# A macaron network of two layers on one core: zero products in the second layer's entry, another order of its tail, and a dispatch that sums on TensorE

## The chip, the core and the metric

The kernel runs on one core of a Trainium2 chip. A core has five engines, each with its own list of instructions that it works through in order: TensorE (PE; its weight loads are listed as PEld), VectorE (DVE), ScalarE (ACT), GpSimd (POOL) and SyncE (SP), which here only issues DMA transfers. The on-chip memory (SBUF) has 128 partitions; TensorE writes to PSUM, used here as eight banks of 128x512 f32. The metric is the device time of one execution in microseconds (us), lower is better.

## The reference

The input is 1024 tokens of 512 features. Two layers follow, each "macaron": half an FFN, an attention, half an FFN again, each behind a layer norm and added to the residual x.

```python
x = x + 0.5 * L0_ffn(layernorm(x))     # mixture: 16 experts, 4 per token, one shared expert
x = x + L0_attn(layernorm(x))          # 32 heads of 16, causal, rope
x = x + 0.5 * L0_ffn(layernorm(x))
x = x + 0.5 * L1_ffn(layernorm(x))
x = x + L1_attn(layernorm(x))          # one head of 128, all to all
x = x + 0.5 * L1_ffn(layernorm(x))

def L0_ffn(x):                         # sigmoid scores, top 4, normed weights cw
    g, u = x @ Wg[e].T, x @ Wu[e].T    # per expert e, 512 -> 256
    out = sum_e ((silu(g) * u) * cw[e]) @ Wd[e].T
    return out + silu(x @ Sg.T) * (x @ Su.T) @ Sd.T

def L1_ffn(x):
    t = x[:, perm].reshape(1024, 16, 32)          # permuted features, 16 heads
    t = gelu(einsum('bhd,hdm->bhm', t, up))       # 32 -> 128 per head
    t = einsum('bhm,hmd->bhd', t, down)           # 128 -> 32
    return t.reshape(1024, 512)[:, argsort(perm)]

def L1_attn(x):                        # q, k, v of 128, softmax, then Wo
    out = softmax(q @ k.T / sqrt(128)) @ v
    return out @ Wo + bo
```

All of it is in f32 (0/1 masks and zeros in narrower types).

## The kernel before, in words

The tokens are eight tiles of 128 (`NT = 8`), and x stays on chip in `x_sb`. A feature-major copy of the normed x is `xT`, made by four 128x128 transposes per tile (`tr`, line 85) into one bank and one copy out of it (`turned`, by ACT). The work of a stage runs as a hand-written order of small units. TensorE's instructions are pinned to that program order (`mm` at line 82, `tr` at line 85). VectorE, GpSimd and ScalarE are pinned as well in the stretches where `order(True)` was called; the wrapper records all their calls at line 99, so line 99 in a profile row can be any of them, and the tile name tells which. Else a scheduler orders them. `bank()` hands out the eight PSUM banks in turn, so a new bank may have to wait until its last reader is done. `idle(n)` issues n products of zeros (bf16, 128x512) that nobody reads.

**The mixture and its dispatch.** A layer's two mixtures, `m0` before and `m1` after layer 0's attention, both work through 35 blocks of up to 2x64 gathered tokens: `gather`, `turn` (transposes and a copy to `xsT`), `gate_up`, `turn_z`, `down`. Ahead of that, `dispatch` (line 1842) works out which token goes to which place: `choose` marks each token's top 4 (`sel`), `spots_mm` (line 471) counts by products of 0/1 matrices, `before` times one tile's `sel` plus `ones` times all earlier tiles', where the sum over tiles before `lo` is read from `cum` (made by `count`, line 457, one VectorE addition per tile); the last column holds the count over all tiles. `counts` turns it into blocks per expert, `experts` and `experts_row` into the expert of each block (`er`), `bases` (line 625) and `blocks_of` (line 637) into each token's block (`pick`, `qh`, then masks `hb`), `invert` by 32 products into the list of tokens by row (`src_i`), which the gathers need. `weights` makes the weighted masks (`hotw`) and, on ACT, f32 casts `hbf` of `hb`; both are read by `invert_weights`, which runs after the first block's second expert product. `rh` is each token's place in its block. Between these steps stand `pieces`, shares of the shared expert's products, as filler on TensorE; the VectorE product that ends each is the `zs` product, put on the list `later`. `first_step` begins with six zero products, then turns the first block and issues the first expert product. In layer 0 dispatch is called at line 1954 with tiles 4 to 7 still to place, for `m1` at line 2061 with only tile 7 left, in the midst of attention's end. SP's queue in layer 0 carries the loads, the stores of the normed tiles (`xn_d`) and the shared expert's weights (`wsh`, issued in round 6, line 1930).

**Layer 1's entry** (lines 1567 to 1593). GpSimd fetches each token's four rows of the mixture's result (`fetch(t)`, four gathers per tile into `yk`). `enter(t)` issues the fetch of tile t+1, adds three rows to x_t on VectorE, norms tile t-1 (`xn`), adds the fourth row, takes tile t's statistics (with one `pow` on GpSimd, which comes behind the fetch in its queue) and turns tile t-1 into `xT`. `permute(t)` applies the feature permutation by 16 products with a 0/1 matrix `pm` (one permutation in what follows) and copies the result to `xp` on ACT. `permuted(t)` transposes `xp` back and rebuilds x_t from it on VectorE in permuted feature order, since layer 1 up to its last FFN keeps x in that order. For tiles 4 and 5 the permutation goes by memory instead: `send` writes xT to `xd`, and `receive` gathers its rows by four DMAs (`xp<-xd`); its place is inside `enter(7)`, between tile 6's norm and tile 7's last addition.

**Layer 1's FFN** (`Ffn1`, line 1383; `f` first, `f2` last). Its columns come in three groups, `GROUPS = ((0, 4), (4, 6), (6, 8))`: tiles 0 to 3 (512 wide), 4 and 5, 6 and 7 (256 wide, the narrow groups). For a group n and one of four chunks i, `up(n, i)` has four products into four banks and four GELUs into tiles `g` (a ring of 12, shared with the output tile `xo`), and `down(n, i)` four products into one bank and a copy into `yT`. In `f2` a `down` starts with one product per tile of x's own 128x128 block by `ident`, which puts x into the sum. The groups 0 and 1 of `f2` return to the original feature order through memory: `yT` is written to `yd`, `fetch` gathers its rows into `xp` (POOL), `back` transposes; group 2 does it by products with `pmt` (`unpermute`). `store` copies to `xo` and writes out.

**Attention of layer 1** (line 1701). For each query tile: scores, a maximum, `probabilities` (exponentials on ACT), `transposed` (the transposes of the probabilities into `pT`, copied by VectorE and ACT), then per half of four tiles `project` (eight products of values with `pT`, copied as `oT`) and `output` (one product with `wo1` per tile; VectorE adds it to x and `after(t)` norms the tile). `turn` then makes xT of the normed tile for `f2`. The first half's outputs and turns 0 to 3 stand on the list `todo` and are worked off among the second half's steps; in the second half's `project` the hook `between[1]` stands after four of the eight products:

```python
        for u in todo:
            u()
        between[0]()                       # f2.up(0, 0)
        oT = project(pT, between[1])       # 4 products, f2.up(0, 1), 4 products
        between[2]()                       # f2.down(0, 0)
        for tt in range(4):
            output(oT, 1, tt)
```

The functions that the change touches, and what calls them:

## Time and profile before

| what | value |
|---|---|
| time, median of 3 runs (lowest, highest) | 1223.39 us (1221.47, 1229.98) |
| the profiled execution: its own time, and the span of its trace | 1225.28 us, 1223.5 us |
| mean granted TensorE clock in it | 0.982 |
| busy, share of the span: PE, PEld, DVE, ACT, POOL | 94%, 44%, 42%, 38%, 25% |
| stretch 24 to 50 us (dispatch of layer 0): PE, DVE, ACT, POOL busy, clock | 20.81, 20.55, 10.33, 6.32 of 26 us, 0.93 |
| stretch 750 to 768 us (second dispatch) | 15.50, 14.45, 9.62, 4.27 of 18 us, 1.00 |
| stretch 1012 to 1077 us (layer 1's entry) | 54.33, 38.37, 19.11, 42.61 of 65 us, 0.92 |
| stretch 1142 to 1223.5 us (end of the last attention, last FFN) | 70.20, 27.98, 33.49, 12.12 of 81.5 us, 0.96 |

How to read the profile: it is one execution, recorded by the hardware. A group of instructions is a line, an engine, an operation, and what it writes and reads by the program's names. In a timeline row the first number is the start in us from the span's start, the second the time from there to the end of the group, then engine, line, operation and tile, shape, count, and in brackets the engine's idle time before it with what ended it. A row of the waits has the waiting instruction, what it waited for, and the sum of the idle us, the count and the longest. A row of a windows view has the window, its length, then busy us (and instruction count) of PE, PEld, DVE, ACT and POOL, the granted TensorE clock (1.00 is full), the DMA share and GB/s. In the slices of the page each digit is the busy share in tenths of one fortieth of the span. Matmuls are pipelined, and their ends are modelled.

### The profile page before, as it was taken

To read this page: it belongs to the slowest core of one execution; us is meant where nothing else is said; L and a number is where in the kernel's file an instruction comes from. 1 tells how busy PE (TensorE), PEld (TensorE's weight loads), DVE (VectorE), ACT (ScalarE), POOL (GpSimd) and SP (SyncE) were. 2 spreads that over 40 slices of the span, in tenths; PEclk is the share of its full clock that TensorE was granted. 3 is DMA by queue.
4 is the path that set the end of the run, shared out by engine and by line. 5 is a ranking of instruction groups with operands and counts; after the bars stand their busy time and mean duration, and the time that the engine had idled before them with its cause. 6 is when DMAs were issued, how large, how long until landed. Compare 5 with 4: busy or idle time off the path is not lost. (4 is left out here: it accounts for less than half of the span.)

```text
span 1223.5 us, 18918 instructions
## 1 busy us (share of the span) xinstructions
PE 1153.5 (94%) x6570; PEld 536.8 (44%) x6570; DVE 515.9 (42%) x1188; ACT 463.0 (38%) x919; POOL 306.1 (25%) x374
## 2 busy tenths in 40 slices
PE   9899999998979999999989998899998998899898
PEld 6643333336544344444433326434333335565544
DVE  6611111115676574746587206531111115755731
ACT  4312222222245545363655693212222221451544
POOL 5211111105355421211101010431121106642002
PEclk9999999999989999999989999999999998999989
DMA  6644567425331200000000002756246615500004
GB/s 242 240 154 147 180 216 268 165 95 150 93 48 28 39 1 10 10 1 10 10 1 9 10 1 97 260 129 214 88 155 248 217 45 148 163 18 1 1 26 147
DMA packets 41973, 125.02 MB, mean 102 GB/s; under 512 B 6240, under 2 KB 8032, under 8 KB 37776
## 3 DMA queue, kind: packets, MB, share of 16 engines
q1 hardware_dynamic: 15680, 58.38, 14.3%
q0 software_dynamic: 14224, 43.34, 13.0%
q10 hardware_dynamic: 11968, 22.02, 4.8%
q8 instruction: 55, 0.90, 0.3%
q14 instruction: 46, 0.38, 0.1%
HBM read 271.69 MB, written 29.62 MB: 246 GB/s over the span
## 5 line engine op out<-in xcount | busy, mean ns | idle before, releaser
L82 PE MATMUL ps<-wg,xsT 128*64 128x512 f32 x1120 | 257.5, 602 | 10.5 <-DMA wg<-in_w_exp_dram 8.3
L99 DVE TENSOR_REDUCE nm<-ps 128x1 f32<-128x512 f32 (+5 forms) x360 | 195.3, 601 | 76.8 <-PE ps L82 76.2
L82 PE MATMUL ps<-kT,qt 32*128 32x512 f32 (+3 forms) x768 | 166.7, 529 | 3.5 <-DVE nm L99 3.3
L1153 ACT ACTIVATE pt<-ps 128x512 f32<-128x512 f32 x224 | 119.3, 602 | 119.7 <-PE ps L82 119.3
L82 PE MATMUL ps<-qt,kT 32*128 32x512 f32 x576 | 153.5, 651 | 0.5 <-DVE nm L99 0.4
L801 POOL DMA_INDIRECT xs<-xn_d,src_i x70 | 68.2, 974 | 319.3 <-PE ps L85 285.0
L82 PEld LDWEIGHTS ps<-wg,xsT 128*64 128x64 f32 x1120 | 75.7, 137 | 142.9 <-issue 137.5
L82 PE MATMUL ps<-wd,zT 128*64 128x512 f32 x560 | 132.5, 593 | 1.0 <-DVE zT L99 1.0
L99 DVE TENSOR_TENSOR z<-sg,ps 128x256 f32<-128x256 f32 x70 | 29.4, 421 | 243.8 <-ACT sg L99 236.2
L99 ACT ACTIVATE sg<-ps 128x256 f32<-128x256 f32 x70 | 26.9, 384 | 256.3 <-PE ps L82 256.3
L862 ACT ACTIVATE y<-ps,w_row 128x512 f32<-128x512 f32 x70 | 48.1, 687 | 105.3 <-PE ps L82 59.3
L82 PEld LDWEIGHTS ps<-kT,qt 32*128 32x128 f32 x768 | 62.9, 184 | 45.4 <-DVE nm L99 14.9
L99 POOL TENSOR_SCALAR_AFFINE_SELECT pt<-pt 128x512 f32<-128x512 f32 x64 | 41.0, 665 | 165.8 <-ACT pt L1157 155.2
L99 POOL TENSOR_TENSOR rstd<-rstd,mhalf 128x1 f32<-128x1 f32 x40 | 23.7, 594 | 234.7 <-DVE rstd L99 230.0
L82 PE MATMUL ps<-pt,va 128*32 128x512 f32 x576 | 78.7, 612 | 0.0
L82 PEld LDWEIGHTS ps<-wd,zT 128*64 128x64 f32 x560 | 40.6, 137 | 78.6 <-issue 76.5
L99 POOL DMA_INDIRECT yk<-y_d,row_i x48 | 49.2, 1026 | 95.4 <-SPq L914 82.4
L99 DVE COPY zT<-ps 128x256 f32<-128x256 f32 x70 | 29.6, 423 | 102.5 <-PE ps L85 102.4
L82 PEld LDWEIGHTS ps<-qt,kT 32*128 32x128 f32 x576 | 49.3, 187 | 52.4 <-issue 23.8
L82 PE MATMUL ps<-xT,wsh 128*128 128x256 f32 x256 | 60.3, 390 | 4.6 <-PEq L914 3.1
L82 PEld LDWEIGHTS ps<-xT,wsh 128*128 128x128 f32 x256 | 48.3, 193 | 14.3 <-issue 4.5
L85 PEld LDWEIGHTS ps<-ident,xs 128*128 128x128 f32 x280 | 29.4, 141 | 56.7 <-issue 54.4
(265 smaller groups left out, 1468.8 us busy)
## 6 DMA issues: line engine op xcount, KB each, us to landing
wg<-in_w_exp_dram SPq DMA_DIRECT2D x142, 1024.0 KB
wd<-in_w_exp_dram SPq DMA_DIRECT2D x142, 512.0 KB
y_d<-y ACTq DMA_DIRECT2D x70, 256.0 KB
xn_d<-xn SPq DMA_DIRECT2D x16, 256.0 KB
wsh<-in_w_exp_dram SPq DMA_DIRECT2D x2, 1536.0 KB
y_d<-y ACTq DMA_DIRECT2D x2, 1280.0 KB
out_dram<-xo SPq DMA_DIRECT2D x8, 256.0 KB
wqkv_sb<-in_w_qkv_dram POOLq DMA_DIRECT2D x2, 768.0 KB
```

The lines of the kernel that those rows point to most:

```text
L82: pin(nc.tensor.matmul(dst, lhsT=lhsT, rhs=rhs, start=start, stop=stop))
L85: pin(nc.tensor.transpose(dst, src, ident))
L99: ins = f(*a, **k)
L801: nc.gpsimd.indirect_dma_start(out=xs, out_offset=None, in_=self.xn_d, in_offset=bass.IndirectOffsetOnAxis(ap=self.src_i[:, s : s + 1], ax ...
L862: nc.scalar.activation(y, py, AF.Copy, scale=self.w_row[:, s : s + 1])
L1153: nc.scalar.activation(pt, pas[j], AF.Exp, scale=1.0 / 16.0)
```

## The change

Eight edits, in the order in which the kernel runs.

- Dispatch. In layer 0 the four additions `count(0, 4)` go, and TensorE sums `ones` times `sel` over all earlier tiles instead of reading `cum` (`spots_mm(..., summed=False)`); in both layers the sum over all tiles is issued first. The `pick` product of `bases` moves from VectorE to GpSimd and right behind `experts`. The masks `hb` are four instructions instead of two, and stand ahead of one `zs` product. ACT's casts `hbf` move behind `first_step`. One piece instead of two stands ahead of layer 0's dispatch, so one more is left for its end.
- The shared expert's weights are loaded in round 5 instead of 6.
- Entry. 28 zero products instead of 14, eight more after `permute(0)`, two more in each of three rounds.
- `receive()` stands behind tile 7's statistics instead of ahead of its last addition.
- `f2`: x is no longer added by products with `ident`. `raw(t)` transposes x_t into a bank and copies it to `xr` (ACT for even, VectorE for odd tiles), and `down` adds `xr` on VectorE in place of its copy.
- `g` and `xo` share ten buffers instead of twelve.
- `oT` is copied by ACT instead of VectorE.
- The tail's order: ahead of the second half's values stand only the outputs of the first half and `raw(0)`, `raw(1)`; then the eight values products without a hook, turns 0 and 1, the second half's outputs, turns 2 and 3, and from there `f2` with its `raw` units spread among `up` and `down`. The third group's `up` and `down` alternate one step further apart.

```diff
@@ -468,22 +468,24 @@
-        def spots_mm(self, lo, hi):
+        def spots_mm(self, lo, hi, summed=True):
...
             def add(at, hi):
-                mm(at, ones, self.cum[:, lo, :], False, hi == lo)
-                for t in range(lo, hi):
+                if summed:
+                    mm(at, ones, self.cum[:, lo, :], False, hi == lo)
+                for t in range(lo if summed else 0, hi):
                     mm(at, ones, self.sel[:, t, :], False, t == hi - 1)
-            for t in range(lo, hi):
-                at = pos[:, bass.ts(t - lo, E)]
-                mm(at, before, self.sel[:, t, :], True, False)
-                add(at, t)
             if hi == NT:
...
                 add(at, NT - 1)
+            for t in range(lo, hi):
+                at = pos[:, bass.ts(t - lo, E)]
+                mm(at, before, self.sel[:, t, :], True, not (summed or t))
+                add(at, t)
             return pos
@@ -626,27 +628,26 @@
             pick = dp.tile(full, F32, tag="pick", name="pick")
-            vec.tensor_mul(
+            pool.tensor_mul(
                 pick, self.oh, self.base.unsqueeze(1).unsqueeze(2).to_broadcast(full)
             )
+            self.based = pick
+        def blocks_of(self, dp):
             bk = dp.tile([P, TOPK, NT], F32, name="bk")
-            vec.tensor_reduce(bk, pick, AX.X, ALU.add)
+            vec.tensor_reduce(bk, self.based, AX.X, ALU.add)
             self.qh = dp.tile([P, TOPK, NT], FP16, name="qh")
...
-        def blocks_of(self, dp):
-            self.hbs = []
-            full = [P, 2, NT, NH]
-            for i in range(2):
-                hb = dp.tile(full, FP16, name=f"hb{i}")
+            self.hbs = [dp.tile([P, 2, NT, NH], FP16, name=f"hb{i}") for i in range(2)]
+            full = [P, NT, NH]
+            for k in range(TOPK):
                 vec.tensor_tensor(
-                    hb,
-                    iota_h[:, 0:NH].unsqueeze(1).unsqueeze(2).to_broadcast(full),
-                    self.qh[:, 2 * i : 2 * i + 2, :].unsqueeze(3).to_broadcast(full),
+                    self.hbs[k // 2][:, k % 2],
+                    iota_h[:, 0:NH].unsqueeze(1).to_broadcast(full),
+                    self.qh[:, k, :].unsqueeze(2).to_broadcast(full),
                     ALU.is_equal,
                 )
-                self.hbs.append(hb)
@@ -700,7 +701,7 @@
             vec.tensor_reduce(wk, pick, AX.X, ALU.add)
-            self.hotw, self.hbf = [], []
+            self.hotw = []
             full = [P, 2, NT, HB]
@@ -708,6 +709,10 @@
+        def blocks_cast(self, dp):
+            self.hbf = []
+            for i in range(2):
                 hf = dp.tile([P, 2, NT, NH], F32, name=f"hbf{i}")
@@ -1407,7 +1412,7 @@
             for pa in pas:
-                g = self.xpool.tile([P, 512], F32, tag="g", name="g", bufs=12)[:, :w]
+                g = self.xpool.tile([P, 512], F32, tag="g", name="g", bufs=10)[:, :w]
                 nc.scalar.activation(g, pa[:, :w], AF.Gelu)
@@ -1418,21 +1423,20 @@
             pb = bank()
+            for j, g in enumerate(self.gs.pop((n, i))):
+                mm(pb[bass.ts(j, 32), :w], late["down"][:, i * 4 + j, :], g)
             if self.last:
-                lo, hi = GROUPS[n]
-                for t in range(lo, hi):
-                    mm(
-                        pb[:, bass.ts(t - lo, P)], x_sb[:, t, bass.ts(i, P)], ident,
-                        t == lo, False,
-                    )
-            for j, g in enumerate(self.gs.pop((n, i))):
-                mm(pb[bass.ts(j, 32), :w], late["down"][:, i * 4 + j, :], g, not self.last, True)
-            if self.last and n:
-                nc.vector.tensor_copy(yT[:, i, :], pb[:, :w])
+                nc.vector.tensor_add(yT[:, i, :], pb[:, :w], self.xr[:, i, self.cols(n)])
             else:
...
+        def raw(self, t):
+            (nc.vector.tensor_copy if t % 2 else nc.scalar.copy)(
+                self.xr[:, :, bass.ts(t, P)], transposes(x_sb[:, t, :])
+            )
@@ -1464,7 +1468,7 @@
         def store(self, t, ps):
-            xo = self.xpool.tile([P, H], F32, tag="g", name="xo", bufs=12)
+            xo = self.xpool.tile([P, H], F32, tag="g", name="xo", bufs=10)
             (nc.vector.tensor_copy if t % 2 else nc.scalar.copy)(xo, ps)
@@ -1542,7 +1546,7 @@
-            def enter(t, *between):
+            def enter(t):
@@ -1550,11 +1554,11 @@
                     entry_apply(t - 1)
-                for u in between:
-                    u()
                 if t < NT:
...
                     entry_stats(t)
+                if t == 7:
+                    receive()
                 if t > 0:
@@ -1568,13 +1572,15 @@
                 u()
-            idle(14)
+            idle(28)
             enter(1)
             permute(0)
+            idle(8)
             for t in range(2, 5):
...
                 permute(t - 1)
+                idle(2)
             f.up(0, 0)
@@ -1588,7 +1594,7 @@
             f.down(0, 3)
-            enter(7, receive)
+            enter(7)
             permute(6)
@@ -1647,22 +1653,41 @@
         f2 = Ffn1(True, xpool, xT)
+        rp = ctx.enter_context(tc.tile_pool(name="xr", bufs=1))
+        f2.xr = rp.tile([P, KC, S], F32, name="xr")
...
+        def amid():
+            f2.raw(0)
+            f2.raw(1)
+        def turns():
+            turn(0)
+            turn(1)
...
             after,
-            [lambda: f2.up(0, 0), lambda: f2.up(0, 1), lambda: f2.down(0, 0)],
+            [amid, turns],
         )
+        turn(2)
+        turn(3)
+        f2.up(0, 0)
+        f2.raw(2)
+        f2.raw(3)
+        f2.up(0, 1)
+        f2.down(0, 0)
         f2.up(0, 2)
...
         f2.down(0, 2)
+        f2.raw(4)
+        f2.raw(5)
         f2.up(1, 0)
@@ -1671,26 +1696,28 @@
         f2.up(1, 2)
+        f2.raw(6)
         f2.down(1, 1)
         f2.up(1, 3)
+        f2.raw(7)
         f2.up(2, 0)
         f2.down(1, 2)
+        f2.up(2, 1)
         f2.down(1, 3)
         f2.fetch(1, xp)
-        f2.up(2, 1)
+        f2.up(2, 2)
         f2.down(2, 0)
+        f2.up(2, 3)
+        f2.down(2, 1)
         for t in (0, 1):
             f2.store(t, f2.back(t, xp))
-        f2.up(2, 2)
         f2.unpermute(2, 0)
-        f2.down(2, 1)
-        f2.up(2, 3)
+        f2.down(2, 2)
         f2.unpermute(2, 1)
+        f2.down(2, 3)
         for t in (2, 3):
             f2.store(t, f2.back(t, xp))
-        f2.down(2, 2)
         f2.unpermute(2, 2)
-        f2.down(2, 3)
         for t in (4, 5):
@@ -1774,14 +1801,12 @@
-        def project(pT, amid=nothing):
+        def project(pT):
             pb = bank()
...
                 mm(pb, v[:, kt, :], pT[:, kt, :], kt == 0, kt == NT - 1)
-                if kt == NT // 2 - 1:
-                    amid()
             oT = ap2.tile([P, 512], F32, tag="oT", name="oT")
-            nc.vector.tensor_copy(oT, pb)
+            nc.scalar.copy(oT, pb)
             return oT
@@ -1827,19 +1852,19 @@
                     todo.extend([lambda tt=tt: output(oT, 0, tt) for tt in range(4)])
-                    todo.extend([lambda t=t: turn(t) for t in range(4)])
...
         between[0]()
-        oT = project(pT, between[1])
-        between[2]()
+        oT = project(pT)
+        between[1]()
         for tt in range(4):
...
-    def dispatch(m, dp, lo, mid, fill, later, rows):
+    def dispatch(m, dp, lo, mid, fill, later, first, rows):
@@ -1848,11 +1873,12 @@
-        pos = m.spots_mm(lo, NT)
+        pos = m.spots_mm(lo, NT, not first)
         m.choices(mid, NT)
...
         pe = m.experts(dp)
+        m.bases(dp)
         for u in rows:
@@ -1862,10 +1888,9 @@
         m.numbers(lo, NT)
-        m.bases(dp)
         pieces(2)
+        m.blocks_of(dp)
         later.pop(0)()
-        m.blocks_of(dp)
         pieces(3)
@@ -1877,6 +1902,7 @@
         m.first_step()
+        m.blocks_cast(dp)
         m.back_rows(dp)
@@ -1926,7 +1952,7 @@
                     stats(t)
-                if t == 6:
+                if t == 5:
                     m0.load_shared(sp)
@@ -1940,18 +1966,16 @@
             pos = m0.spots_mm(0, 4)
-            m0.count(0, 4)
             compare(6)
...
             choose(6)
-            for _ in range(2):
-                z.pop(0)()
+            z.pop(0)()
...
-            dispatch(m0, dp, 4, 4, z, later, [rows])
+            dispatch(m0, dp, 4, 4, z, later, True, [rows])
             for eng in (vec, pool, act):
@@ -2058,7 +2082,7 @@
             m1.choose(t, NT, m1.compare(t, NT, vec))
-            dispatch(m1, dp, t, t, m1_z[:12], m1_later, [])
+            dispatch(m1, dp, t, t, m1_z[:12], m1_later, False, [])
             del m1_z[:12]
```

## The prediction

> **What bounds the kernel now.** One core, five engines, each running its own list in order. I first read the page's busy shares and slices.
>
> ```profile
> span 1223.5 us, 18918 instructions
> ...
> PE   9899999998979999999989998899998998899898
> ...
> PEclk9999999999989999999989999999999998999989
> ```
>
> TensorE (PE) is busy almost everywhere, so only a stretch where PE idles, runs at a lower granted clock, or does work that can be left out is worth anything. The change touches three: the two dispatches (24 to 50 us and 750 to 768 us), layer 1's entry (1012 to 1077 us) and the tail (1142 us to the end). I read the timeline of each, and the granted clock by windows where PE had idled. First the dispatch of layer 0, on VectorE (DVE), ScalarE (ACT) and PE:
>
> ```profile
> 24.25 1.60 DVE L99 TENSOR_TENSOR cum<-cum,sel 128x16 bf16<-128x16 bf16 x4
> 36.19 0.68 DVE L99 TENSOR_TENSOR pick<-oh,base 128x512 f32<-128x512 bf16 x1
> 46.57 2.41 ACT L99 CAST hbf<-hb 128x1280 f32<-128x1280 f16 x2
> 48.88 0.59 ACT L99 COPY xsT<-ps 128x512 f32<-128x512 f32 x1
> 49.52 3.65 PE L82 MATMUL ps<-wg,xsT 128*64 128x512 f32 x16 [1.54 <-ACT xsT L99]
> ```
>
> The first expert product waits for a copy that stands behind two casts; before that, a chain of small DVE steps decides. Next the clock (PEclk is the third column from the right, after the busy times) and the entry:
>
> ```profile
> 1030.00:1032.00 2.00, 1.33 (x6) 0.93 (x5) 1.77 (x5) 0.58 (x1) 1.39 (x3) 0.50 0.67 209
> 1048.00:1050.00 2.00, 2.00 (x11) 2.00 (x11) 1.93 (x5) 0.00 (x0) 1.39 (x3) 0.50 0.65 213
> 1166.00:1168.00 2.00, 2.00 (x9) 0.50 (x2) 0.00 (x0) 1.14 (x3) 0.00 (x0) 0.50 0.04 8
> ```
>
> ```profile
> 1031.22 6.36 PE L82 MATMUL ps<-xT,pm 128*128 128x128 f32 x32 [0.67 <-issue]
> ...
> 1071.13 0.98 POOL L99 DMA_INDIRECT xp<-xd,pcol  x1 [3.40 <-DMA xd<-xT]
> ...
> 1072.86 3.84 PE L82 MATMUL ps<-xT,pm 128*128 128x128 f32 x32 [0.67 <-ACT xT L99]
> ...
> 1076.51 0.55 DVE L99 TENSOR_SCALAR xn<-x_sb,mvs,rstds 128x512 f32<-128x512 f32 x1 [5.56 <-issue]
> ```
>
> The same permutation takes 6.36 us at clock 0.50 and 3.84 us at 1.00. DVE's waits in 1028 to 1078 us name the victim:
>
> ```profile
> DVE x_sb L99 <- PE ps L85: 7.3, 3, 3.2
> ```
>
> Last, PE's timeline of the tail, and the windows view of 1158.10 to PE's last product (busy PE first):
>
> ```profile
> 1159.16 1.27 PE L85 MATMUL ps<-ident,xn 128*128 128x128 f32 x8 [1.06 <-DVE xn L99]
> 1163.40 1.09 PE L85 MATMUL ps<-ident,xn 128*128 128x128 f32 x4 [2.97 <-DVE xn L99]
> 1165.16 2.09 PE L82 MATMUL ps<-xT,up 32*128 32x512 f32 x8 [0.67 <-ACT xT L99]
> 1167.18 4.91 PE L82 MATMUL ps<-pT,v 128*128 128x512 f32 x8
> ...
> 1173.10 3.70 PE L82 MATMUL ps<-pT,v 128*128 128x512 f32 x8
> ...
> 1187.58 0.66 PE L85 MATMUL ps<-ident,xn 128*128 128x128 f32 x4
> ...
> 1190.96 1.16 PE L82 MATMUL ps<-ident,x_sb 128*128 128x128 f32 x8
> 1158.10:1219.23 61.13, 54.88 (x348) 27.73 (x348) 18.29 (x41) 28.50 (x66) 11.45 (x15) 0.94 0.22 74
> ```
>
> PE waits for four normed tiles, its clock halves, and the next products run at half pace. Afterwards it is the bound.
>
> **Dispatch, layer 0: 2.2 us.** Four additions to cum leave: 1.60 us, stretched while GpSimd (POOL) subtracted at 24.12 to 25.22. The following steps can start at about 24.5 instead of 25.77: 1.2. The sum over all tiles goes first on PE: eight products at 0.027 us instead of nineteen before it: counts start 0.4 sooner. 15 more such products (0.4 us) stand before filler that nobody waits for. The 0.68 us product goes to POOL, where the like 128x512 subtraction took 1.04; DVE's next small steps run just then. A DVE TENSOR_SCALAR of 0.54 us took 1.50 at 1092.70 beside a POOL addition, so I count this move as nothing (between -0.4 and +0.7).
>
> The Trainium skill says the same more strictly ("SBUF — State Buffer", section "SBUF: two separate sides"): the port pair is an exclusive lock, and a DVE instruction with two SBUF inputs or in a two-port mode blocks fully against a reading POOL instruction. The additions' 1.60 us agrees. By the rule the move costs up to 0.4 us, so 1.8 us here instead of 2.2.
>
> One zs product goes behind the block masks: 0.33. The masks come in four parts, so the inversion's last wait covers 8 products and not 16: 0.36. Together 2.3 us earlier at the row numbers. Then PE has six filler pieces instead of five (0.9 each): -0.9; and the xsT copy no longer stands behind the casts (48.88 against PE's end at 48.0): +0.85. About 2.2; I bound it by 0.6 (mask inputs late from ACT, whose table load now stands among them) and 3.0. The casts, 2.41 us, move beside the second expert product (3.65 us); were that cover gone, the weight inversion would wait up to 2.4. The shared weights' DMA passes two stores on SP's queue: it ends a 1.47 us wait of PE that lay beside DVE's chain, and the stores are read 18 us later. Nothing.
>
> Layer 1's dispatch: PE works without a gap from 754.0 through filler and inversion to 764, so the DVE steps saved are hidden, and xsT was copied 0.03 us after its transposes anyhow: 0 (-0.3 to +0.5).
>
> **Entry: 4.5 us.** 28 zero products instead of 14 (14 took 3.25 us) end at 1029.4, inside the 3.03 us that PE waited for xn. Eight more (1.7 us) fall between 1035.1 and the next xn at 1037.0; two per round (0.43) mostly before xn. So the clock should hold: permutation 0 ends at 1035.1 instead of 1037.6, 1 starts at 1038.3 and takes 3.84 where the xp copy came 5.7 us after its start, 2 takes 3.84 instead of 5.47, 3 follows at 1049.5 and not 1053.3. The FFN's first products then start at 1054.0 instead of 1058.56. Is this allowed? POOL issues the yk gathers, 1.28 us apart with one power per tile, without a break until 1051: its pace holds, and tiles up to 4 come no sooner. Tile 5's power moves from 1058.5 to 1057.1, tile 6's from 1066.8 to about 62.6, behind gathers. From 1054.0 ACT is busy for 13.7 us (table 1.28, 16 GELUs at 0.515, copies), so permutation 6 starts at 1068.4 instead of 1072.86: 4.5. The receive (four gathers, behind a 3.40 us wait for xd) now stands after tile 7's power on POOL: DVE's 5.56 us wait goes, worth only 0.4 us on PE. Its first gather lands by 1070 and is needed at 1073. From 1077 to 1128 PE is 51.41 of 51.50 us busy, so the gain passes on. If the 1.8 and 0.8 us by which permutations 1 and 3 were slow at a recorded clock of 1.0 stay: 1.9. The high end is 4.9.
>
> The clock rows come first here: idles of 3.0, 2.0 and 3.0 us were each followed by 3.4 or 6.8 us at 0.50. The skill ("TensorE: Matmul & The Clock Gate", "What's actually happening") puts a re-throttle after one whole idle window of about 3.4 us; here a window only about half busy sufficed, and by the rule alone the 2.0 us idle would not have counted, making the entry gain some 1.5 us smaller.
>
> **Tail: 9.5 us.** The second half's values no longer wait for tiles 0 to 3: two raw transposes fill PE, the last pT copy on DVE is due at 1160.1, values run at full clock to 1167. PE's work from 1158.1 by start-to-start times, before: values 8x0.875, outputs 4x0.87, ups 9.0, downs 8.6, unpermuting 8x0.87, transposes 13x0.44, x products 8.3: 49.1. Idle 61.13-54.88 = 6.25, half clock 2.6 (4.91-3.70, 2.09-1.14, 1.09-0.66), rest 3.2. After: minus 8.3, plus 8 raw transposes 3.5, one output and one turn that come later now 1.3: 45.6. New waits, going through the built order: 0.4 for pT, 1.0 for xT of tiles 2 and 3 behind the outputs, 0.1, and 1.6 where the third hidden group needs a bank that a GELU still holds: 3.1 to 3.6. With a rest of 3.0 to 3.2 PE ends at 1157.8+45.6+3.4+3.1 = 1209.9 instead of 1219.2: 9.3 to 9.5. VectorE's additions (0.69 like its 512-wide copies) replace copies of ACT; the oT copy on ACT starts 0.1 sooner. The yd gathers start 2.7 us after the last yT copy as before, and land 0 to 1 us before they are read. With ten g buffers instead of twelve the third GELU of a narrow group waits for the product after it: about 0.3 us, mostly within PE's pace of 1.4 per pair. Bounds: 6 (ACT paces) to 12.5 (no rest).
>
> **Sum.** 2.2+0+4.5+9.5 = 16.2. The profiled execution took 1225.28 us (span 1223.5, 1.8 around it): 1209.1. The median of the runs, 1223.39, is 1.9 lower: 1207.2. I say 1207.5.
>
> **Rivals.**
> Entry and dispatch hidden (12%): POOL's unbroken gathers speak for it, DVE's 7.3 us of waits against. Left is the tail: 1223.4-9.5 = 1213.9.
> Tail paced by ACT (12%): GELUs 18 us, table 1.3 and copies against; ACT is only 28.50 of 61.13 us busy. 1223.4-6.7-6 = 1210.7, or 1213 with a smaller entry.
> Slower (6%): the g ring. Sixteen narrow groups (eight per FFN) each wait for the product behind them. At 0.3 us hidden; if each loses 1.0 us on PE, the 16.2 are gone, and at 1.3 us the time is 1223.4-16.2+20.8 = 1228. Against: PE needs each GELU only two groups later.
> The change doesn't hold the clock (5%): half clock in the entry as before, 1223.4-11.7 = 1211.7.
>
> **How the numbers follow.** Forecast 65%. About 1% is what a measurement of this kernel tells from no change; its lower edge is 1211.2. The forecast lies under it save a tenth, the ACT case mostly, the hidden entry above: faster 0.74, same 0.20, slower 0.06. Range: all high ends (3.0+0.5+4.9+12.5) give 1202.5, a little lower by the runs' spread: 1201; the hidden entry 1213.9, to 1215.
>
> **What would show it.** Right: permutations near 3.84 us and clock 1.00 from 1024 on; tile 7's power ahead of the xp gathers; no PE wait over 1.7 us after the last probabilities; no half clock there; the first expert product 2 us earlier. Wrong: DVE still waiting 7 us for PE in the entry, er later on DVE beside POOL's pick, PE waiting for g in narrow groups, or the yd gathers ending the tail.

## The result, and the profile after

The changed kernel takes 1219.18 us in the median of 20 executions (1213.02 to 1231.35), the kernel before 1226.05 us in 20 beside them: a ratio of 0.9936 (0.9917 to 0.9956). It is faster by 7 us, not by 16: the time lies above the stated range of 1201 to 1215.

```profile
span 1220.6 us, 18961 instructions
...
PE   8999999999879999999989998899999899899998
...
PEclk9999999999989999999989999999999999999999
```

The last two dips of the clock (PEclk), those of layer 1's entry and of the tail, are gone from the slices, as forecast; the two further left stand where they stood. TensorE is as busy as before. To see where the time went I cut each profile at the starts of TensorE groups that both kernels have. Read from the timelines (us), with the second column the same cut's mean over the profiles, of this kernel and of the experiments below, that have the part in its old or new form (4 to 11 profiles for each form; the one with the lowest clock, 0.972, is left out, and a kernel that has a part half in the old and half in the new form does not count for that part):

| stretch | before, after | old form, new form (mean) | forecast |
|---|---|---|---|
| start to the first expert product | 49.52, 48.12 | 49.6, 48.4 | -2.2 |
| that to the second mixture's dispatch (`sel` product) | 701.31, 706.54 | 705.5, 704.1 | 0 |
| dispatch to its fifth expert product | 53.77, 59.91 | 55.3, 60.9 | 0 |
| fifth to last expert product | 199.41, 197.24 | 197.1, 197.4 | 0 |
| last expert product to the last attention's first values product | 137.79, 136.35 | 135.9, 135.1 | -4.5 |
| that to TensorE's end | 77.43, 68.37 | 78.1, 68.5 | -9.5 |

The means add up to -1.2 - 1.4 + 5.6 + 0.3 - 0.8 - 9.6 = -7.1. The tail came as forecast. The second dispatch costs 5.6 us that the forecast put at nothing, and the entry, forecast at 4.5, gives about 1; single profiles of the new entry lie between 131.5 and 138.2 us, so that this 1 is not clear of the scatter.

In layer 0's dispatch (timeline, several engines: start, length, engine, line, operation):

```profile
30.24 1.15 POOL L99 TENSOR_TENSOR pick<-oh,base 128x512 f32<-128x512 bf16 x1 [4.86 <-DVE base L99]
30.58 0.84 DVE L99 TENSOR_SCALAR ends<-ends,part_f 128x16 f32<-128x16 f32 x1
...
48.12 3.65 PE L82 MATMUL ps<-wg,xsT 128*64 128x512 f32 x16 [0.68 <-ACT xsT L99]
```

The pick product runs on GpSimd right over VectorE's small `ends` step, which takes 0.84 us. The second dispatch shows the same step with and without it (before, then after):

```profile
753.11 0.23 DVE L99 TENSOR_SCALAR ends<-ends,part_f 128x16 f32<-128x16 f32 x1
...
753.70 0.38 PE L82 MATMUL ps<-ident,eid 128*1 128x128 f32 x2 [0.79 <-DVE eid L99]
760.25 1.35 PE L82 MATMUL ps<-hb,hotv 128*64 128x80 f16 x32
...
775.31 3.65 PE L82 MATMUL ps<-wg,xsT 128*64 128x512 f32 x16 [0.94 <-DMA wg<-in_w_exp_dram]
```

```profile
756.63 1.15 POOL L99 TENSOR_TENSOR pick<-oh,base 128x512 f32<-128x512 bf16 x1 [7.08 <-ACT hotv L99]
756.95 0.87 DVE L99 TENSOR_SCALAR ends<-ends,part_f 128x16 f32<-128x16 f32 x1
...
758.17 0.38 PE L82 MATMUL ps<-ident,eid 128*1 128x128 f32 x2 [1.42 <-DVE eid L99]
764.72 1.33 PE L82 MATMUL ps<-hb,hotv 128*64 128x80 f16 x32
...
781.39 5.10 PE L82 MATMUL ps<-wg,xsT 128*64 128x512 f32 x16 [2.54 <-DMA wg<-in_w_exp_dram]
```

The `ends` step takes 0.64 us longer, and TensorE waits 1.42 us for `eid` instead of 0.79. TensorE's filler stands behind `eid`'s product, so the filler, the inversion, the plan (`plan`: for SP, the expert of each block) and SP's request for the second block's weights are all late by the same 0.63 us, counted from the dispatch's first product. GpSimd's gathers of the first blocks' tokens are not: they come only 0.11 us later (12.10 us against 11.99), and the first expert product comes in time (16.98 against 16.95). The second block's weights come 2 us late, and its product, the last row of each view, with them (26.73 against 24.48). With the request late and the gathers in time the third gather now goes out ahead of the request, where it used to go out behind it (timelines of SP and GpSimd, before and then after):

```profile
765.27 1.03 SPq L780 DMA_DIRECT2D wg<-in_w_exp_dram  x2
765.44 0.95 POOL L801 DMA_INDIRECT xs<-xn_d,src_i  x1 [0.30 <-issue]
```

```profile
769.41 0.95 POOL L806 DMA_INDIRECT xs<-xn_d,src_i  x1 [0.30 <-issue]
769.73 1.03 SPq L785 DMA_DIRECT2D wg<-in_w_exp_dram  x2
```

The entry's permutations, and the zero products between them:

```profile
1040.54 0.60 PE L85 MATMUL ps<-ident,xn 128*128 128x128 f32 x4
1041.81 3.84 PE L82 MATMUL ps<-xT,pm 128*128 128x128 f32 x32 [0.68 <-ACT xT L99]
1045.48 1.89 PE L82 MATMUL ps<-zero 128*128 128x512 bf16 x8
...
1065.64 2.00 PE L82 MATMUL ps<-xp,up 32*128 32x512 f32 x16 [0.24 <-ACT xp L99]
```

These rows are at full clock; 3.4 us of half clock lie ahead of them, from 1023 us on, behind a wait of 2.02 us that the section on the bank below shows. TensorE's waits in the tail (what waits, for what, sum, count, longest):

```profile
PE ps L85 <- DMA xp<-yd,ucol: 2.0, 1, 2.0
PE ps L82 <- ACT xT L99: 0.7, 1, 0.7
PE ps L82 <- ACT oT L1809: 0.7, 1, 0.7
PE ps L85 <- ACT pr L1785: 0.6, 1, 0.6
PE ps L82 <- DVE xr L1437: 0.5, 1, 0.5
```

The 4.7 us that TensorE waited for `xn` there in the kernel before, and the half clock behind it, are gone; this profile has a wait of 2.0 us for the `yd` gathers that the one of before lacks (two other profiles with the old tail have 1.3 and 1.4 us of it).

### The profile page after: what moved, and what is told of

Read it like the earlier page. It is cut to its first block, busy times and chain, and to the rows that moved or that the text cites. A ratio compares the mean times of both kernels' runs of the same rounds, so it can differ in the third digit from the quotient of the medians.

```text
span 1220.6 us, 18961 instructions
## 1 busy us (share of the span) xinstructions
PE 1155.5 (95%) x6581; PEld 534.2 (44%) x6581; DVE 519.3 (43%) x1192; ACT 463.8 (38%) x921; POOL 308.6 (25%) x376
## 5 line engine op out<-in xcount | busy, mean ns | idle before, releaser
L82 PE MATMUL ps<-wg,xsT 128*64 128x512 f32 x1120 | 262.5, 610 | 10.1 <-DMA wg<-in_w_exp_dram 8.7
L82 PEld LDWEIGHTS ps<-wg,xsT 128*64 128x64 f32 x1120 | 77.5, 139 | 145.7 <-issue 137.9
L82 PEld LDWEIGHTS ps<-qt,kT 32*128 32x128 f32 x576 | 49.5, 187 | 53.3 <-issue 23.8
L85 PEld LDWEIGHTS ps<-ident,xs 128*128 128x128 f32 x280 | 29.4, 141 | 56.7 <-issue 55.1
```

The source lines that it names most:

```text
L82: pin(nc.tensor.matmul(dst, lhsT=lhsT, rhs=rhs, start=start, stop=stop))
L85: pin(nc.tensor.transpose(dst, src, ident))
```

## Experiments

The time of one kernel's executions varies by some 10 to 20 us, nearly in line with the mean clock that was granted: over 286 of the executions here, 1.09 us per 0.001 of clock (correlation -0.89). So beside the ratio I give each kernel's mean time at a clock of 0.982, moved along that slope; by the scatter within a set of executions, the error of such a mean is 0.3 to 1.0 us. Between sets it can be larger: the kernel before stands at 1223.9 to 1224.0 in the sets beside `e1` to `e12` and at 1225.0 in the set beside `e13` to `e16`, and one kernel, taken twice (`e12`, `e16`), differs by 5.8. The full change stands at 1220.3.

**The same two kernels again, and the dispatch taken out or alone.** (The branch in the table's last column is `m1.rest()`: it skips a body of further blocks.) No edit in the first two; the others are the diff's dispatch hunks undone (`e3`) or done alone (`e4`).

> The changed kernel once more, unedited, for a second profile and the clocks of more executions. Its first profile had five windows at half clock that the one of before lacks (at 184, 283, 781, 805 and 1023 us; 17 us together), each behind a wait of TensorE of 2.0 to 2.5 us. Theory A (chance): where such a window falls is settled anew in each execution, so most of the five are at other places or absent, and the time varies by some 5 us with the mean clock. Theory B (dispatch): the windows at 781 and 805 us and the 2.5 us wait for wg ahead of them come back, since the new dispatch puts the second mixture's first transfers elsewhere. Theory C (code): the 2.0 us wait of TensorE behind the second mixture's skipped branch (0.33 us before) comes back to 0.1 us, since it hangs on the instruction list alone. Entry and tail as in the first profile: 3.84 us per permutation, values to the end of TensorE 68.4 us by all three.

> The kernel before once more, unedited, for the clocks of its executions and a second profile. Theory A: its windows outside entry and tail (343, 627, 688, 716, 948 us) are joined by others in some executions, and its mean clock varies as much as that of the changed kernel, about 0.976 to 0.984; the ones in entry and tail come back. Theory B: no window at the first blocks of the second mixture. Theory C: 0.33 us behind the second mixture's branch again.

> Entry and tail as changed, both dispatches, the shared weights' load and the number of filler pieces as before. My sum gives 14.0 us less than before here, and 2.2 us more than the full change. Theory A: the measured gain over before is within 3 us of the full change's 7, and smaller by 1 to 2. Theory B: it is larger than the full change's by 4 us or more (11 to 14), since the second mixture's first blocks are as before. Theory C: as A, but decided by the wait behind the branch: 2.0 us again if the entry's or the tail's code sets it, 0.33 if the dispatch's does.

> The kernel before with the dispatch part alone (sums on TensorE, pick on GpSimd, four masks, later casts, earlier shared weights, one more filler piece at the end). Prediction: 2.2 us less than before. Theory A: 0 to 2 less, within the runs' spread. Theory B: 4 to 7 us more than before, with the second mixture's first weights late by 1.6 us more than before and half clock behind. Theory C: no opinion on the time; the wait behind the second branch changes from 0.33 us if the dispatch's code sets it.

| run | ratio (interval) | at clock 0.982 | 5 blocks of the second mixture | last expert product to the branch's first product |
|---|---|---|---|---|
| changed, again | 0.9943 (0.9911, 0.9976) | 1220.5 | 45.4 | 10.21 |
| before, again | 1.0002 (0.9966, 1.0039) | 1223.5 | 40.0 | 8.53 |
| old dispatch | 0.9905 (0.9871, 0.9938) | 1216.5 | 39.2 | 8.53 |
| dispatch alone | 1.0006 (0.9977, 1.0036) | 1225.7 | 43.6 | 10.21 |

Theory A explains part: of the five extra windows at half clock only the one at 184 us came back in place, those at 781 and 805 came back as 777 and 801, those at 283 and 1023 did not; but the last one, behind theory C's wait, comes at the same place in three later profiles (`e10`, `e11`, `e13`). Theory B stands: the second mixture's start is slow in each profile with the new dispatch and in none without (42.9 to 45.4 us for its first five blocks against 36.8 to 41.2, the experiments further below included). And theory C's wait comes back to the hundredth, and goes with the dispatch, which does not touch that code.

**The pick product on VectorE, later on GpSimd, and the second dispatch in the old order.**

```diff
# e7: in bases, called where it was before
-            pool.tensor_mul(pick, ...)
+            vec.tensor_mul(pick, ...)
# e10: bases called behind experts_row
+            vec.tensor_copy(base, self.base)   # a new tile, read by the product
             pool.tensor_mul(pick, self.oh, base ...)
# e9: in dispatch, for the second mixture only
+        if not first: bases (pick on vec) behind numbers; the zs product
+            ahead of blocks_of; blocks_cast ahead of first_step
```

> The full change, with the pick product on VectorE and at its old place, all else as changed. Theory B1 (the product on GpSimd slows the small VectorE step that makes eid): eid's TensorE product is back at 2.87 us behind the dispatch's first product in the second mixture (3.51 with the product on GpSimd), the inversion at 9.42 instead of 10.06, the second block's weights are asked for 0.63 us sooner, and its first product starts at 24.5 to 25.0 instead of 26.5 to 27.0; the time is 2 to 5 us under the full change. Theory B2 (the later casts or the four masks cause the late weights): eid back, but the second block still at 26 or later, and the time within 1 us of the full change.

> The full change, with the pick product still on GpSimd but released 0.6 us later: it reads a copy of base that VectorE makes behind er. Theory B1 (it is the overlap with the one small step that leads to eid): eid back at 2.87 us, the second block's first product at 24.5 to 25.0 behind the dispatch's first product, although the product runs on GpSimd. Theory B3 (any work of GpSimd's there holds the chain up): the stretch moves to a later small step, the inversion stays at 9.42 since TensorE's filler covers it, or comes up to 0.6 us later.

> The full change, with the second mixture's dispatch in the old order (pick on VectorE at its old place, the zs product ahead of the masks, the casts ahead of the first expert product; the four narrower masks stay); layer 0's dispatch, entry and tail as changed. Theory B (the second dispatch costs 4 to 6 us): the second mixture's first five blocks take 37 to 40 us (full change 42.9 and 45.4; pick alone moved back 40.3), the weights of its second block are waited for under 1 us; 5 to 8 us under the full change, 10 to 14 under before. Theory A (chance): within 2 us of the full change. The wait behind the branch is 0.33 us by the bank that this version gets.

With the product moved back, and with it left on GpSimd but released 0.6 us later, `eid` is at 2.87 and 2.88 us and the inversion at 9.42 in both. The timeline of the second of these:

```profile
753.38 0.23 DVE L99 TENSOR_SCALAR ends<-ends,part_f 128x16 f32<-128x16 f32 x1
...
753.97 0.38 PE L82 MATMUL ps<-ident,eid 128*1 128x128 f32 x2 [0.79 <-DVE eid L99]
755.11 1.16 POOL L99 TENSOR_TENSOR pick<-oh,base 128x512 f32<-128x512 bf16 x1 [9.11 <-DVE pickp L99]
```

The product moved later meets another step, and theory B's delay with it: VectorE's cast of `pp`, 0.17 us elsewhere, takes 0.94 here and ends with the product:

```profile
755.35 0.94 DVE L99 CAST pi<-pp 128x4 int32<-128x4 f32 x1
```

Filler on TensorE hides that one, and the inversion is not later for it. So which step the product holds decides whether `eid` is late. It does not decide alone whether the second block is: that comes at 25.2 us with the product on VectorE and at 26.5 with the later one (before 24.5, full change 26.7), and the first five blocks take 40.3 and 43.4 us. The second pair was a miss of the expectation. In `e10` the weights are asked for in time (14.43 us, as in `e7`) and still land late: the product waits 1.74 us for them. What `e10` has in common with the full change is the order of the requests. Its gathers start 0.5 us sooner than in `e7` (11.47 against 11.97 us), and the third again goes out ahead of the weights' request:

```profile
765.20 0.95 POOL L808 DMA_INDIRECT xs<-xn_d,src_i  x1 [0.30 <-issue]
765.52 1.03 SPq L787 DMA_DIRECT2D wg<-in_w_exp_dram  x2
```

All 18 profiles divide by this order: in the seven with the third gather ahead of the request the second block comes at 26.5 to 27.1 us, in the other eleven at 24.2 to 25.2. No run changes this order alone, so that the order is the reason is argued, not shown. With the old order in the second mixture (`e9`) its first five blocks took 40.8 us, a wait of 0.80 us for weights, and the ratio is 0.9905 (0.9866 to 0.9945), 1217.9 at equal clock; `e7` is at 0.9951 (0.9922 to 0.998) and 1220.4, `e10` at 0.9947 (0.9914 to 0.998) and 1218.0. That `e7` gains nothing overall against the full change I can't explain by the dispatch; its entry took 3 us more than the mean (138.2 against 135.1), one draw.

**Another bank behind the branch.**

```diff
+            idle(1)                 # one zero product
             m1.blocks(extra)
         m1.rest()
```

> The full change with one more zero product (0.22 us) ahead of the second mixture's blocks. It shifts which PSUM bank the first product behind the skipped branch gets: in the full change one whose last reader is an instruction of ScalarE inside the skipped body, so that TensorE waits until ScalarE has passed the branch; here one that was read for the last time ahead of it, as in the kernel before. Theory C1 (the bank decides): the stretch from the last expert product to the first product behind the branch is 8.53 us instead of 10.21, no half clock behind it, and the time is 1.5 to 3.5 us under the full change. Theory C2 (instruction fetch decides): 10.2 us stay.

```profile
1019.74 7.15 PE L82 MATMUL ps<-xT,wsh 128*128 128x256 f32 x32 [0.33 <-PEq L919]
```

In the full change the same row, the first behind the branch, is

```profile
1022.02 8.86 PE L82 MATMUL ps<-xT,wsh 128*128 128x256 f32 x32 [2.02 <-ACTq L919]
```

The stretch is 8.53 us again: the bank decides. (The full change's 32 products take 8.86 us and not 7.15, since 3.4 us of half clock fall into them.) In the instruction lists of the programs the first product behind the branch has bank 0 in the kernel before and waits for ScalarE's 731st count, which is reached ahead of the branch; in the full change it has bank 1 and waits for the 741st, which ScalarE adds only when it has passed the branch; here it has bank 4 and waits for the 731st again. The scheduler hands out banks in an order that the dispatch's edits shift. The time was a miss: 0.9967 (0.994 to 0.9993), 1222.3 at equal clock. In this profile the entry's zero products stall twice (0.65 and 0.98 us) and TensorE waits 2.03 us instead of 0.68 for the first copy of `xT`, with nothing that the profile names as the cause, so the first permutation came no sooner.

**Entry alone, tail alone.** The hunks of `enter`, `idle` and `receive`; those of `Ffn1`, `attention1` and the order of `f2`.

> The kernel before with the entry part alone (more zero products, receive behind tile 7's statistics). The prediction says 4.5 us less than before, from one execution whose entry held 10 us at half clock. Rival: in other executions of kernels with the old entry only 3.4 us of half clock fell there, so the part is worth 0 to 2 us in the median; no permutation at 6.4 us here, and from the second mixture's last expert product to the last attention's values 132 to 134 us, against 137.8, 133.5 and 134.3 with the old entry.

> The kernel before with the tail part alone (values without the wait for tiles 0 to 3, x transposed and added by VectorE, ten g buffers, oT by ScalarE, new order). The prediction says 9.5 us less than before. From the first values product to TensorE's end: 67.3 to 68.4 us as with the full change, against 77.4 to 79.2 before, so 9 to 11 us less in the median. Rival (the g ring or ScalarE paces it): 72 us or more. If the loss of the full change comes from the dispatch, the second mixture's first five blocks take 37 to 40 us here (before 36.8 and 40.0) and TensorE waits 0.33 us behind the branch.

The tail alone: 0.9937 (0.9909 to 0.9965), 1218.7; 68.75 us to TensorE's end, as expected. The entry alone is slower than before: 1.0039 (1.0005 to 1.0072), 1228.8. No permutation at 6.4 us, as expected, but the first one took 5.47 us, with half clock in it, and came 3 us late: ScalarE's first copy of `xT` started 2.6 us after its transposes, again with no named cause. So this run does not tell what the entry's part is worth without that stall.

**x by TensorE's products in the new order.**

```diff
# in down, for f2
+                for t in range(lo, hi):
+                    mm(pb[...], x_sb[:, t, bass.ts(i, P)], ident, t == lo, False)
-                nc.vector.tensor_add(yT[:, i, :], pb[:, :w], self.xr[...])
# raw, xr and all calls of raw left out
```

> The full change, with x put into the last sums by TensorE's products with ident as before (no raw transposes, no xr; groups 1 and 2 copied by VectorE, group 0 by ScalarE), in the new order. By my terms the products cost 8.3 us and the raw transposes 3.5, so 4.8 us of the tail's 9.5 go: from the first values product to TensorE's end 72 to 74 us against 68.2 and 68.4. Rival: TensorE waits elsewhere in the full change, and the difference is under 3 us; or the values now wait without the raw transposes as cover, and it is 6 or more.

69.79 us to TensorE's end against 68.5 on the mean: 1.3 us, a miss of my 4.8, and 0.9946 (0.9916 to 0.9975). Counted start to start, the products take 9.0 us here and the raw transposes 3.9 in the full change, so the term was right. But the full change then waits: 0.5 us for `xr`, 2.0 for the gathers of `yd`, and its `up` groups take 1.0 us more (10.8 against 9.8). Of the other eleven profiles with the new tail five have a wait for these gathers (0.9 to 2.2 us); the six without it have longer `up` groups instead (11.7 to 12.3 us). Neither wait is here:

```profile
PE ps L82 <- ACT xT L99: 0.9, 2, 0.7
PE ps L82 <- ACT oT L1804: 0.7, 1, 0.7
PE ps L85 <- ACT pr L1780: 0.6, 1, 0.6
PE ps L82 <- DVE pT L1794: 0.3, 1, 0.3
```

**Zero products and receive.** `e12` is `e9` with the zero products of before, `e13` the full change with them, `e14` the kernel before with `receive` moved and nothing else, `e15` tail and `receive` alone, `e16` is `e12` again.

```diff
-            idle(28)
+            idle(14)
...
-            idle(8)
...
-                idle(2)
```

> As the version with the second dispatch in the old order, but with the zero products of before (14, none, none); receive stays behind tile 7's statistics. Prediction's term: without them the first permutations run at half clock, 3 to 5 us more. By the profiles since (old entry 126.9 us from the second mixture's end to the last attention's values on the mean, new 126.2): within 1.5 us of the version with them, with half clock in the entry in some executions.

> The full change with the zero products of before (14, none, none). If the added zero products cost what they take (14 behind the first permutation, 3.0 us, and 14 ahead of it that only fill a wait): 2 to 4 us less than the full change at equal clock (1216.5 to 1218.5 against 1220.4), and from the first permutation to the last attention's values 103 to 105 us with half clock counted at full rate (105.4 with them). Rival (they hold the clock as predicted): 3 to 5 us more, with half clock in the entry in most executions.

> The kernel before with receive behind tile 7's statistics, nothing else. In the prediction this was worth 0.4 us. From the profiles: VectorE's wait of 5.6 us in enter(7) goes; if that holds the permutation of tile 6 up, 1 to 3 us less than before at equal clock (1221 to 1223). Rival: within 0.5 us of before.

> Tail and receive as changed, both dispatches and the zero products as before. If layer 0's new dispatch is worth the 1.4 us by which its first expert product came sooner: 1.4 us above the version that has it (1210.7 at equal clock), so 1212. If the first mixture's later waits for weights take that back: 1210 to 1211. If the old zero products alone made that version fast: both 5 to 6 us under the tail alone (1218.7).

> Once more the version with layer 0's new dispatch, the second mixture's old one, the zero products of before, receive behind tile 7's statistics, and the new tail. 1207 to 1213 us and a ratio to before of 0.983 to 0.989 if its six executions were typical; 0.990 (as with the new zero products) if they were a lucky set. Its second profile: second mixture's first five blocks 37 to 39 us.

| run | ratio (interval) | executions | at clock 0.982 |
|---|---|---|---|
| e12 | 0.9852 (0.982, 0.9883) | 6 | 1210.7 |
| e13 | 0.9952 (0.9922, 0.9982) | 12 | 1219.0 |
| e14 | 1.0004 (0.9965, 1.0042) | 12 | 1223.5 |
| e15 | 0.9924 (0.9889, 0.9959) | 12 | 1217.8 |
| e16 | 0.9914 (0.9881, 0.9946) | 12 | 1216.5 |

The first and the last are one kernel, and repeated it gives 0.9914, not 0.9852. That is more than chance among executions: moved to equal clock, the first set's six lie between 1209.2 and 1213.6 us and all twelve of the second above them, between 1214.4 and 1220.2. In the two profiles the gap lies in the entry, 131.2 against 139.7 us, of which 3.4 are half clock; most of the rest is one idle of TensorE in `e16`, 5.10 us ahead of the FFN's first products (0.68 in `e12`), for which the profile names no cause. So a set can differ by some 6 us from another set of the same kernel, and what is said here of single versions by 1 to 5 us is not clear of that.

With the old zero products the full change is at the same ratio as with them (0.9952 against 0.9936 and 0.9943); at equal clock it is 1.3 us lower, and its clock was lower by some 0.003, which costs it 3. That the new zero products buy clock and cost time, in nearly equal parts, would fit this pair; but `e9`, which has them, lies in clock between `e12` and `e16`, which lack them (0.983; 0.984 and 0.979), so it is not shown. `receive` alone is worth nothing, as forecast (0.4). Layer 0's new dispatch shows in `e16` against `e15` as 1.3 us, inside their errors. The versions with the old second dispatch and the new tail (`e3`, `e6`, `e9`, `e12`, `e15`, `e16`) lie between 0.985 and 0.994. At equal clock these six stand at 1210.7 to 1218.7 us, and the five with the new second dispatch and the new tail (the full change twice, `e8`, `e11`, `e13`) at 1219.0 to 1222.3: the groups do not overlap, if only just, and their means differ by 4.4 us. This is how the second dispatch shows in the whole time, in four of the five with the wait behind the branch. Of the six `e3`, the full change with the old dispatches, is the plainest version that beats both kernels: 0.9905 over 12 executions, and 1216.5 at equal clock, where the full change stands at 1220.3.

## Why the prediction was wrong

**Right.** The tail's size: 9.5 forecast, 9.6 on the mean, and no half clock in it in the changed kernel's two profiles (3.4 us in four of the ten others with the new tail). Permutations at 3.84 us, the FFN's first products 22.8 us behind the first permutation (23.8 and 23.5 in two profiles), the permutation of tile 6 at 37.2 us (37.6, 37.2): from the first permutation on, the entry after the change is as I drew it. `receive` at about nothing.

**Wrong: "Layer 1's dispatch ... 0 (-0.3 to +0.5)".** This step failed. I had seen the row where a VectorE step of 0.54 us took 1.50 beside GpSimd, and netted the pick product's move to nothing, since VectorE's own list became shorter. But I argued that TensorE works without a gap from the filler on, and drew only half of it: what VectorE saves behind `eid` is hidden by the filler, and what it loses ahead of `eid` is not, since the filler itself starts behind `eid`. The stretched step passes in full (0.63 us) to the request for the second block's weights, and the sign that I had named against me, `er` later beside POOL's product, came. The product back on VectorE, all else left as changed, brings the five blocks from 42.9 to 45.4 back to 40.3 us (`e7`), so the other edits of the dispatch cost little or nothing there. Together with the half clock that follows such waits the stretch measures +5.6. Why the weights come 2 us late where their request is 0.63 us late is open. In `e10` they come as late though they are asked for in time, so a late `eid` is not all of it; the order of the third gather and the request fits all 18 profiles, and I had not thought of it.

**Wrong: the entry's gain.** 4.5 us was read as the difference to one execution of before, in which two dips of the clock (6.8 and 3.4 us) fell into the entry. The profiles with the old entry have 3.4 to 10.2 us of half clock there and take 133.5 to 137.9 us, 135.9 on the mean: 1.9 of the 4.5 were the sample. (By the rule that the prediction quotes for the clock, the idle of 3.0 us, under 3.4 too, would not have counted either; the trace decides.) The rest went ahead of the first permutation. From the last expert product to it the old entry takes 27.1 us, the new one 29.0. I had laid the 28 zero products into the 3.03 us that TensorE waited for `xn` in one execution, and with that wait filled, what is late ahead of them passes on. The wait behind the branch shows it: with the old entry (`e4`) it is absorbed, 27.3 us; with the new one the first permutation comes at 26.6 and 27.1 us without the wait (`e3`, `e9`), at 28.3 with it (`e1`), and at 30.0 where half clock follows the wait (full change, `e10`, `e11`). In the remaining three (`e5`, `e7`, `e8`: 29.4 to 30.0) the stalls without a named cause take the time. From the first permutation to the values it is 108.8 against 106.0: the clock holds in seven of nine profiles and 2.8 us are gained, where I had 4.5. VectorE still waits 7.4 us for TensorE's transposes there, which I had named as a sign against me.

**Half right: layer 0's dispatch.** 2.2 forecast, 1.4 in this profile and 1.2 on the mean. `ends` took 0.84 us there too, a loss of 0.6, more than the 0.4 that I had allowed for the move at worst and the nothing that I took. That this is the whole of the difference is not shown: `e7`, with the product back on VectorE, has its first expert product at 48.60 us, no sooner, with 6.8 us of half clock ahead of it. The Trainium skill ("SBUF — State Buffer", "SBUF: two separate sides") says that a VectorE instruction with two SBUF inputs, or in a two-port mode, blocks in full against a GpSimd instruction that reads SBUF. The rows agree that VectorE waits to the end: `ends` ends at 31.42 where the product beside it ends at 31.39, at 757.82 beside 757.78 in the second mixture, and the cast of `e10` at 756.29 beside 756.27. In these three rows the step is as long as what is left of the product, though 0.17 to 0.23 us elsewhere; the cast of one element (`steps`, 1x1) took its 0.14 us beside it. Whether a step falls under the rule by its inputs or by its mode no run shows.

**The rivals.** The nearest was the hidden entry, 1213.9, and the entry did lose most of its gain, but, as far as the profiles show, not by GpSimd's gathers. A tail paced by ScalarE did not come; of a slower g ring there are waits of TensorE for `g` of 0.2 to 0.8 us in the tails of three profiles; half clock in the entry behind the first permutation came in two of nine.

**Right sum, other parts: the tail.** x on VectorE frees 5 us of TensorE, as counted, and gives back nearly 4 of them in waits and longer `up` groups; in this profile the largest wait is for gathers whose lead I had at 0 to 1 us. The order (values without the wait for tiles 0 to 3) brings the rest: 78.1 to 69.8 us with the products still in.

**Not foreseen:** the bank behind the branch, 1.7 us, from edits elsewhere, and 1.7 more where half clock follows it (four of the seven profiles that have the wait, none of the others). It is shown in its own stretch, not in the whole time.

**Open.** In some profiles ScalarE or TensorE stands for 2 to 5 us in the entry with its inputs ready and nothing named as the cause (`e5`, `e7`, `e8`, `e13`, `e16`). Why is open. One such stall is most of what separates the profiles of `e12` and `e16`, which are one kernel.

## What to carry to other kernels

When work moves to an engine that runs beside another, look for the smallest step on the critical chain that it will overlap, not for the sum of the work: here 0.64 us on a step of 0.23 cost more than all that the move saved. Filler on the bounding engine hides savings behind it and passes on every delay ahead of it. When one request is late and its neighbours are not, look at what now goes out ahead of it. Take the gain of a step that removes a disturbance from several executions, or halve it: the profile shows one draw. Take a set of executions twice before a difference of a few us between sets is believed.

## What the hardware showed unexpectedly

Half-rate stretches of the clock come in multiples of 3.4 us (3.4 to 13.7 in these profiles), some behind idles of only 2 us: the wait of 2.02 us behind the branch was followed by one in four of seven profiles. Where they fall explains most of the spread between executions of one program: 1.09 us per 0.001 of mean clock over 286 executions. A count that an engine adds only after passing a branch made TensorE wait 2.02 us instead of 0.33, by the choice of one PSUM bank. A transfer of weights landed 2 us later in the seven profiles in which a third gather was issued 0.3 us ahead of it, and not in the eleven in which it was issued behind it; that the order is the reason is not shown.
